# A fifth batch's first half by seven block products, and one of its block sums made by two DMA loads

## The chip, the cores and the metric

One core of one Trainium2 chip runs the whole program. The metric is the device time of one execution in microseconds; the median of the runs shown counts. Everything is in float32 with matmuls of split operands, as described below.

## The reference

The input `x` has 8 batches of 1024 rows and 512 columns; `cond` has one row of 512 per batch. Two layers, each with a residual, follow each other:

```python
# L0: a layer matrix with a low-rank part that depends on the batch
ae = _layernorm(ada_emb, ln_g, ln_b)
h = gelu(ae @ w1 + b1, approximate=False)
x_a, x_b = split(h @ w2 + b2, 2)           # per batch: 512 x 8 each
layer = base_layer[None] + einsum('bdr,bkr->bdk', x_a, x_b)
x = x + einsum('btc,bco->bto', x, layer)
# L1: a matrix scaled by the condition on both sides
ys = y / sqrt(512)
d = rsqrt(einsum('bi,io->bo', ys * ys, weight * weight) + 1e-8)
x = x + einsum('bsi,io->bso', x * ys[:, None, :], weight) * d[:, None, :]
```

So each batch's output is its 1024x512 block of `x` times one 512x512 matrix, P_b.

## The kernel before

The kernel first makes the eight matrices P_b (in the code `q[b]`, and `ph[b]`, `pl[b]` split in two), and then multiplies. Each float32 operand is split into a rounded high part (ScalarE casts it) and the rest (VectorE, DVE in the profile, subtracts), and a product is three matmuls: high x high, high x rest, rest x high.

A batch has two halves of 512 rows, a half has four tiles of 128. The common way is `main(b, t)`: one tile of 128 rows is twelve 128x512 matmuls (`po`), an eviction by ScalarE (`o`) and a store on ScalarE's queue. The halves' inputs come in by `load_x` on SyncE's queue (1 MB), are split by `split_x` into `xs`, and the matrices are split by `split_p`.

The last halves are done in another way, by the class `Seven`: a half is cut in 2x2 blocks, and seven block products replace eight (Winograd's scheme). `make_sums` makes the right sums T1 to T4 of one batch's matrix (tile `traw`, rounded to `th`, rests in `tl`), `make_right` splits the matrix itself, and `make_left` makes the left sums S1 to S4 of one half (`sraw`, `sh`, `sl`) and the split blocks `xa` and `x22`. The raw sums of both kinds share one buffer, with the tag `sums`. `part(g, steps, ...)` issues the seven products in the order 1, 5, 6, 2, 7, 3, 4, the evictions between them, and after each product one step of the generator `make_left` of the next half, so that the next half is prepared while this one is multiplied. The PSUM banks are named `sw`, `sz` and `sv` in the profile. The bank `sw` holds product 1, and products 6, 7 and 4 are added onto it; the sum after product 6 is copied out by ScalarE, the one after product 7 is added by DVE, the one after product 4 is copied by ScalarE:

```python
            for p in self.ORDER:
                key = {5: "z", 3: "z", 2: "v"}.get(p, "w")
...
                    if p == 1:
                        se.copy(bank["v"][0][:, to], u)
                    elif p in (3, 7):
                        ve.tensor_add(o[:, to, cols], u, o[:, to, cols])
                    else:
                        se.copy(o[:, to, cols], u)
```

Before the change, five halves go by `Seven`: the second half of batch 5 (called 5_1 here) and both halves of 6 and 7. 44 tiles go by `main`: tiles 0 to 43, where tile i is batch i // 8, tile i % 8 of it.

What runs beside a tile is written down by hand: `at(*place(i), f, ...)` puts a step behind tile i. While `InOrder.on` is false, which it is from the first tile to the last, a scheduler may reorder the steps on ScalarE and DVE by priority; within the parts of `Seven` they stand as written. Each engine then runs its queue in order. SyncE carries the x loads and the stores of the parts, ScalarE the stores of the tiles, GpSimd (POOL) small loads earlier in the program.

Of the kernel before, what the change touches and what calls it, by code (L numbers as in the profile page):

```python
# [7 lines left out]
F32 = mybir.dt.float32  # L8
F32R = mybir.dt.float32r
AF = mybir.ActivationFunctionType  # L10
ALU = mybir.AluOpType
# [3 lines left out]
P = 128  # L15
NB = 8
# [14 lines left out]
def cond_resid_kernel(ctx: ExitStack, tc: tile.TileContext, small, cond, condrows, consts,  # L31
# [10 lines left out]
    nc = tc.nc  # L42
# [9 lines left out]
    class InOrder:  # L52
# [4 lines left out]
        def __init__(self, engine):  # L57
            self.engine = engine
# [5 lines left out]
    ve, se, sy = InOrder(nc.vector), InOrder(nc.scalar), InOrder(nc.sync)  # L64
# [14 lines left out]
    def big_tile(name, dtype=F32):  # L79
        return big.tile([P, KC, D], dtype, tag="big", name=name)  # L80
# [126 lines left out]
    r, t = newton_rsqrt(ve_l, sd, [NB, 1], "l")  # L207
# [86 lines left out]
    r, t = newton_rsqrt(v, sv, [P, KC, NB], "d")  # L294
# [15 lines left out]
    def work_tile():  # L310
        turns[0] += 1
        return work[:, turns[0] % KC, :]
# [61 lines left out]
    a11, a21 = b_raw[:, 0:2, 0:HD], b_raw[:, 0:2, HD:D]  # L374
    a12, a22 = b_raw[:, 2:4, 0:HD], b_raw[:, 2:4, HD:D]
# [158 lines left out]
    fold, pools = {}, {}  # L534
# [184 lines left out]
    def load_x(b, h):  # L719
        raw[b, h] = big_tile(f"x_{b}_{h}")  # L720
        sy.dma_start(raw[b, h], x[b, h])

    def split_x(b, j, part=None):

        t = raw[b, j // 2][:, :, (j % 2) * 2 * P:(j % 2 + 1) * 2 * P]
        if part != 1:
            xs[b, j] = big.tile([P, 2, KC, 2 * P], F32R, tag="big", name=f"xs_{b}_{j}")
            se.copy(xs[b, j][:, 0], t)
        if part != 0:
            hi, lo = xs[b, j][:, 0], xs[b, j][:, 1]  # L730
            ve.tensor_sub(lo, t, hi.bitcast(F32))
# [49 lines left out]
    two = Pair(2, False)  # L781
# [123 lines left out]
    class Seven:  # L905
# [9 lines left out]
        ORDER = (1, 5, 6, 2, 7, 3, 4)  # L915

        def __init__(self, b):
            self.b, self.left, self.right = b, {}, {}

        def make_sums(self):  # L920

# [32 lines left out]
                                  (3, slice(2, 4), slice(HD, D))):  # L954
                self.right[p] = ph[b][:, rows, cols], pl[b][:, rows, cols]

        def make_left(self, g):

            b, late = self.b, pools["late"]
            top, low = (raw[b, g][:, :, 2 * P * i:2 * P * (i + 1)] for i in range(2))  # L960
            a11, a12, a21, a22 = top[:, 0:2], top[:, 2:4], low[:, 0:2], low[:, 2:4]
            s = late.tile([P, 4, 2, 2 * P], F32R, tag="sl", name=f"sl_{b}_{g}", bufs=2)
            h = late.tile([P, 4, 2, 2 * P], F32R, tag="sh", name=f"sh_{b}_{g}", bufs=2)
            x = late.tile([P, 2, 2, 2 * P], F32R, tag="x22", name=f"x22_{b}_{g}", bufs=2)
            xa = big.tile([P, 2, KC, 2 * P], F32R, tag="big", name=f"xa_{b}_{g}")
            raws = late.tile([P, 4, 2, 2 * P], F32, tag="sums", name=f"sraw_{b}_{g}", bufs=1)
            s1, s2, s3, s4 = (raws[:, i] for i in range(4))
            self.left[g] = {5: (h[:, 0], s[:, 0]), 6: (h[:, 1], s[:, 1]), 7: (h[:, 2], s[:, 2]),
                            3: (h[:, 3], s[:, 3]), 4: (x[:, 0], x[:, 1]),
                            1: (xa[:, 0, 0:2], xa[:, 1, 0:2]), 2: (xa[:, 0, 2:4], xa[:, 1, 2:4])}  # L970

            def rest(two):
                ve.tensor_sub(s[:, two], raws[:, two], h[:, two].bitcast(F32))

            se.copy(xa[:, 0], top)
            se.copy(x[:, 0], a22)
            ve.tensor_add(s1, a21, a22)
            ve.tensor_sub(s2, s1, a11)
            yield
            se.copy(h[:, 0:2], raws[:, 0:2])  # L980
            ve.tensor_sub(s3, a11, a21)
            ve.tensor_sub(s4, a12, s2)
            yield
            se.copy(h[:, 2:4], raws[:, 2:4])
            ve.tensor_sub(xa[:, 1], top, xa[:, 0].bitcast(F32))
            yield
            rest(slice(0, 2))
            yield
            ve.tensor_sub(x[:, 1], a22, x[:, 0].bitcast(F32))
            yield  # L990
            rest(slice(2, 4))
            yield

        def product(self, g, p, banks, first):
# [53 lines left out]

    def late_pools():
        making.close()  # L1050
        pools["o"] = ctx.enter_context(tc.tile_pool(name="opool2", bufs=3))
        pools["late"] = ctx.enter_context(tc.tile_pool(name="late", bufs=1))

    NTT = NT // P
    after = {}

    def at(b, t, f, *args):
        after.setdefault((b, t), []).append((f, args))
# [5 lines left out]
    place = lambda i: divmod(i, NTT)  # L1064
# [9 lines left out]
    for b, spots in ((4, [11 + n for n in spread]), (6, [21 + n for n in spread])):  # L1074
# [3 lines left out]
        for n, p in enumerate(Pair.ORDER):  # L1078
            spot = spots[2 * n]
# [14 lines left out]
    def all_left(seven, g):  # L1094
        for _ in seven.make_left(g):
# [12 lines left out]
    TILES = (NB - 2) * NTT - NTT // 2  # L1108
    for i in range(TILES):
        b, t = divmod(i, NTT)  # L1110
        if t == 0 and b + 1 < NB - 2:
# [86 lines left out]
```

## Time and profile before

| what | value |
|---|---|
| median of 3 runs | 294.06 us (293.88 to 294.23) |
| profiled execution | 293.74 us, of it the span 291.9 us |
| TensorE busy | 286.3 us, 98% of the span |
| DVE, ScalarE, GpSimd busy | 214.8, 175.0, 35.9 us |
| granted TensorE clock | 0.998 |

The span is what the trace shows, from the first instruction to the last; the time of an execution is 1.84 us longer. All times below in the form 226.94 are microseconds from the span's start. In a group of the profile, `out<-in` names the tiles by the program's names with the numbers left out, and a time in brackets is how long the engine had been idle and what it waited for. Instructions issued through the helpers `mm` and `InOrder` all stand at the helper's line, so they are told apart by their tiles.

### The profile page before, as it was taken

To read this page: it belongs to the slowest core of one execution; us is meant where nothing else is said; L and a number is where in the kernel's file an instruction comes from. 1 tells how busy PE (TensorE), PEld (TensorE's weight loads), DVE (VectorE), ACT (ScalarE), POOL (GpSimd) and SP (SyncE) were. 2 spreads that over 40 slices of the span, in tenths; PEclk is the share of its full clock that TensorE was granted. 3 is DMA by queue.
4 is the path that set the end of the run, shared out by engine and by line. 5 is a ranking of instruction groups with operands and counts; after the bars stand their busy time and mean duration, and the time that the engine had idled before them with its cause. 6 is when DMAs were issued, how large, how long until landed. Compare 5 with 4: busy or idle time off the path is not lost.

```text
span 291.9 us, 4100 instructions
## 1 busy us (share of the span) xinstructions
PE 286.3 (98%) x1519; PEld 225.2 (77%) x1519; DVE 214.8 (74%) x295; ACT 175.0 (60%) x272; POOL 35.9 (12%) x77
## 2 busy tenths in 40 slices
PE   7999999999999999999999999999999999999995
PEld 3665566467877878888877888887888889999994
DVE  2889898989916999519799565326789977798912
ACT  5757263286849884658654575544658745856641
POOL 2111000202944560000022000000000000000000
PEclk9999999999999999999999999999999999999999
DMA  7999999992799783332328114262175870852334
GB/s 209 405 429 413 411 403 405 390 383 90 187 321 322 235 250 116 110 145 93 159 80 263 55 72 135 83 216 74 72 251 176 291 257 1 290 204 87 142 146 144
DMA packets 19924, 62.14 MB, mean 213 GB/s; under 512 B 2736, under 2 KB 4016, under 8 KB 15552
## 3 DMA queue, kind: packets, MB, share of 16 engines
q1 hardware_dynamic: 9504, 43.76, 40.7%
q10 hardware_dynamic: 6912, 12.32, 11.5%
q0 software_dynamic: 3488, 5.79, 7.5%
q8 instruction: 12, 0.20, 0.3%
q14 instruction: 8, 0.07, 0.1%
HBM read 44.02 MB, written 17.84 MB: 212 GB/s over the span
## 4 chain that ended last, share of the span: by engine, by line
PE 96%; DMA 2%; ACT 0%; DVE 0%; SPq 0%; ACTq 0%; issue 0%
PE po L45 42%; PE pp L45 20%; PE sw L45 9%; PE px L45 5%; PE sz L45 5%; PE pg L45 4%; PE pq L45 4%; PE sv L45 2%; DMA b_raw<-in_baseT 2%; PE pr L45 1%; PE pt_t L45 1%; PE ps_t L45 0%; PE pq_v L45 0%; PE pq_z L45 0%; ACT o L62 0%; DVE o L62 0%
## 5 line engine op out<-in xcount | busy, mean ns | idle before, releaser
L45 PE MATMUL po<-ph,xs 128*128 128x512 f32 x352 | 113.7, 392 | 0.0
L45 PEld LDWEIGHTS po<-ph,xs 128*128 128x128 f32 x352 | 66.0, 188 | 15.6 <-issue 1.7
L45 PE MATMUL po<-pl,xs 128*128 128x512 f32 x176 | 68.6, 390 | 0.0
L62 ACT COPY o<-po 128x512 f32<-128x512 f32 x44 | 25.9, 588 | 35.0 <-PE po L45 35.0
L45 PEld LDWEIGHTS po<-pl,xs 128*128 128x128 f32 x176 | 33.0, 188 | 6.7
L62 DVE TENSOR_TENSOR xs<-x,xs 128x1024 fp32r<-128x1024 f32 (+1 forms) x23 | 27.0, 1176 | 15.0 <-ACT xs L62 15.0
L62 DVE TENSOR_TENSOR nl_p<-n,nh_p 128x1024 fp32r<-128x1024 f32 x21 | 25.7, 1222 | 12.4 <-ACT nh_p L62 12.4
L62 ACT CAST nh_p<-n 128x1024 fp32r<-128x1024 f32 x21 | 22.1, 1054 | 14.6 <-DVE n L62 10.9
L62 ACT CAST xs<-x 128x1024 fp32r<-128x1024 f32 x22 | 23.0, 1056 | 3.6 <-DMA x<-in_x 3.6
L62 ACT COPY q<-pp 128x512 f32<-128x512 f32 x30 | 17.4, 586 | 8.7 <-PE pp L45 8.6
L542 POOL DMA_DIRECT2D fa<-kept_a x28 | 13.8, 508 | 58.3 <-PE pr L45 54.0
L45 PE MATMUL pp<-nh_p,sh 128*128 128x512 f32 x48 | 19.0, 396 | 0.0
L45 PE MATMUL pp<-nh_p,sl 128*128 128x512 f32 x48 | 18.7, 390 | 0.0
L45 PE MATMUL pp<-nl_p,sh 128*128 128x512 f32 x48 | 18.7, 390 | 0.0
L62 DVE SCALAR_TENSOR_TENSOR n<-w_sb,ysT,d 128x512 f32<-128x512 f32 x24 | 16.9, 748 | 0.9 <-DMA d<-d_out 0.9
L62 ACT CAST sh<-sraw 128x1024 fp32r<-128x1024 f32 (+1 forms) x14 | 12.9, 926 | 6.8 <-DVE sraw L62 6.8
L62 DVE TENSOR_TENSOR sl<-sraw,sh 128x1024 fp32r<-128x1024 f32 (+1 forms) x14 | 14.9, 1067 | 2.2 <-ACT sh L62 2.2
L62 DVE TENSOR_TENSOR pl<-q,ph 128x1024 fp32r<-128x1024 f32 (+1 forms) x10 | 11.1, 1116 | 6.9 <-ACT ph L62 6.9
L45 PE MATMUL px<-w,hT 128*32 128x512 f32 x128 | 15.6, 599 | 0.0
L62 ACT COPY o<-sw 128x512 f32<-128x512 f32 (+1 forms) x12 | 6.2, 518 | 15.4 <-PE sw L45 12.3
L62 DVE TENSOR_TENSOR q<-pr,q 128x512 f32<-128x512 f32 x14 | 8.8, 688 | 7.9 <-PE pr L45 7.8
L62 DVE TENSOR_TENSOR n<-n,n 128x1024 f32<-128x1024 f32 x12 | 14.5, 1225 | 0.1
(199 smaller groups left out, 576.6 us busy)
## 6 DMA issues: line engine op xcount, KB each, us to landing
w<-in_w SPq DMA_DIRECT2D x16, 1024.0 KB, 10.4
x<-in_x SPq DMA_DIRECT2D x16, 1024.0 KB, 5.6
out<-o ACTq DMA_DIRECT2D x44, 256.0 KB, 2.3
out<-o SPq DMA_DIRECT2D x8, 512.0 KB, 2.9
fa<-kept_a POOLq DMA_DIRECT2D x28, 64.0 KB, 2.7
ft<-kept_t POOLq DMA_DIRECT2D x28, 64.0 KB, 3.5
d<-d_out POOLq DMA_DIRECT2D x6, 256.0 KB, 7.3
w_sb<-in_w SPq DMA_DIRECT2D x1, 1024.0 KB, 8.5
```

The lines of the kernel that those rows point to most:

```text
L45: tc.keep_in_program_order(nc.tensor.matmul(*args, **kw))
L62: return lambda *a, **kw: pin(f(*a, **kw)) if InOrder.on else f(*a, **kw)
L542: nc.gpsimd.dma_start(fold[name, b][32 * c:32 * c + 32, :], kept[name, g][32 * i:32 * i + 32, :])
```

## The change

The first half of batch 5 (5_0) goes by seven products as well: 40 tiles go by `main`, six halves by `Seven`. The left sum S1 = A21 + A22 of each of the six halves is no longer added by DVE; `load_sum` loads A21 from the input in DRAM to a tile `s1` of its own (one buffer) and then A22 onto it, in an accumulating DMA, both on GpSimd's queue. The load of the next half's S1 is issued within `make_left`, once this half's S1 has been read. The steps of `make_left` are put in another order, with the casts and rests of single sums apart. Batch 5's matrix is split by `make_right` (three quarters of it) rather than `split_p`; the right sums of 5, 6 and 7 are made behind tiles 32, 37 and 38; `make_right` of batch 6 moves into part 5_0. The output tiles in the late stage have two buffers rather than three.

```diff
+        def load_sum(self, g):
+
+            xg = x[self.b, g]
+            s1 = pools["late"].tile([P, 2, 2 * P], F32, tag="s1", name=f"s1_{self.b}_{g}", bufs=1)
+            nc.gpsimd.dma_start(s1, xg[:, 0:2, 2 * P:])
+            nc.gpsimd.dma_start(s1, xg[:, 2:4, 2 * P:], accum_op=ALU.add)
+            self.s1[g] = s1
...
-        def make_left(self, g):
+        def make_left(self, g, following=None):
...
-            s1, s2, s3, s4 = (raws[:, i] for i in range(4))
+            s1, (s2, s3, s4) = self.s1.pop(g), (raws[:, i] for i in range(1, 4))
...
             se.copy(xa[:, 0], top)
             se.copy(x[:, 0], a22)
-            ve.tensor_add(s1, a21, a22)
+            ve.tensor_sub(s3, a11, a21)
+            yield
+            ve.tensor_sub(xa[:, 1], top, xa[:, 0].bitcast(F32))
+            se.copy(h[:, 2], s3)
+            ve.tensor_sub(x[:, 1], a22, x[:, 0].bitcast(F32))
+            yield
+            se.copy(h[:, 0], s1)
             ve.tensor_sub(s2, s1, a11)
             yield
-            se.copy(h[:, 0:2], raws[:, 0:2])
-            ve.tensor_sub(s3, a11, a21)
             ve.tensor_sub(s4, a12, s2)
+            se.copy(h[:, 1], s2)
+            ve.tensor_sub(s[:, 0], s1, h[:, 0].bitcast(F32))
+            se.copy(h[:, 3], s4)
+            if following:
+                following[0].load_sum(following[1])
             yield
-            se.copy(h[:, 2:4], raws[:, 2:4])
-            ve.tensor_sub(xa[:, 1], top, xa[:, 0].bitcast(F32))
+            rest(slice(1, 3))
             yield
-            rest(slice(0, 2))
-            yield
-            ve.tensor_sub(x[:, 1], a22, x[:, 0].bitcast(F32))
-            yield
-            rest(slice(2, 4))
+            rest(slice(3, 4))
             yield
...
-        pools["o"] = ctx.enter_context(tc.tile_pool(name="opool2", bufs=3))
+        pools["o"] = ctx.enter_context(tc.tile_pool(name="opool2", bufs=2))
...
-    for b, spot in ((4, 27), (5, 33)):
-        for j in range(2):
-            at(*place(spot + j), split_p, b, j)
+    for j in range(2):
+        at(*place(27 + j), split_p, 4, j)
...
-    at(*place(34), s5.make_sums)
-    at(*place(34), s5.share_right)
-    at(*place(35), s6.make_sums)
-    at(*place(37), s7.make_sums)
-    at(*place(38), load_x, NB - 3, 1)
-    at(*place(39), all_left, s5, 1)
-    at(*place(41), s6.make_right)
-    at(*place(42), load_x, NB - 2, 0)
-
-    TILES = (NB - 2) * NTT - NTT // 2
+    at(*place(32), s5.load_sum, 0)
+    at(*place(33), load_x, NB - 3, 0)
+    at(*place(32), s5.make_sums)
+    at(*place(34), s5.make_right)
+    at(*place(35), all_left, s5, 0, (s5, 1))
+    at(*place(36), load_x, NB - 3, 1)
+    at(*place(37), s6.make_sums)
+    at(*place(38), s7.make_sums)
+
+    TILES = (NB - 3) * NTT
...
+    load_x(NB - 2, 0)
+    s5.part(0, s5.make_left(1, (s6, 0)), then=s6.make_right)
     load_x(NB - 2, 1)
-    s5.part(1, s6.make_left(0))
+    s5.part(1, s6.make_left(0, (s6, 1)))
     load_x(NB - 1, 0)
-    s6.part(0, s6.make_left(1))
+    s6.part(0, s6.make_left(1, (s7, 0)))
     load_x(NB - 1, 1)
-    s6.part(1, s7.make_left(0), then=s7.make_right)
+    s6.part(1, s7.make_left(0, (s7, 1)), then=s7.make_right)
     s7.part(0, s7.make_left(1))
     s7.part(1, last=True)
```

In the queues as built, the right sums of batches 6 and 7 stand on DVE behind the left sums of 5_0; the casts of 6's are on ScalarE behind the eviction of tile 38; those of 7's stand in part 5_0, behind the `sv` copy of product 1 and ahead of the cast of S3 of 5_1, which itself stands ahead of the copy that follows product 6.

More of the change, by code (lines that the diff above doesn't have):

```diff
@@ L917, in __init__ @@
         def __init__(self, b):
-            self.b, self.left, self.right = b, {}, {}
+            self.b, self.left, self.right, self.s1 = b, {}, {}, {}
+        def load_sum(self, g):
[4 more added lines that the diff above has]
+            self.s1[g] = s1
         def make_sums(self):
@@ L970, in make_left, with rest @@
                             1: (xa[:, 0, 0:2], xa[:, 1, 0:2]), 2: (xa[:, 0, 2:4], xa[:, 1, 2:4])}
-            def rest(two):
-                ve.tensor_sub(s[:, two], raws[:, two], h[:, two].bitcast(F32))
+            def rest(at):
+                ve.tensor_sub(s[:, at], raws[:, at], h[:, at].bitcast(F32))
             se.copy(xa[:, 0], top)
             se.copy(x[:, 0], a22)
-            ve.tensor_add(s1, a21, a22)
+            ve.tensor_sub(s3, a11, a21)
[5 more added lines that the diff above has]
+            se.copy(h[:, 0], s1)
             ve.tensor_sub(s2, s1, a11)
             yield
-            se.copy(h[:, 0:2], raws[:, 0:2])
-            ve.tensor_sub(s3, a11, a21)
             ve.tensor_sub(s4, a12, s2)
+            se.copy(h[:, 1], s2)
[3 more added lines that the diff above has]
+                following[0].load_sum(following[1])
             yield
-            se.copy(h[:, 2:4], raws[:, 2:4])
-            ve.tensor_sub(xa[:, 1], top, xa[:, 0].bitcast(F32))
+            rest(slice(1, 3))
             yield
-            rest(slice(0, 2))
-            yield
-            ve.tensor_sub(x[:, 1], a22, x[:, 0].bitcast(F32))
-            yield
-            rest(slice(2, 4))
+            rest(slice(3, 4))
             yield
@@ L1087, in cond_resid_kernel, with all_left @@
         at(*place(end + 1), rank_term, b + 1)
-    for b, spot in ((4, 27), (5, 33)):
-        for j in range(2):
-            at(*place(spot + j), split_p, b, j)
+    for j in range(2):
+        at(*place(27 + j), split_p, 4, j)
     s5, s6, s7 = (Seven(NB - i) for i in (3, 2, 1))
-    def all_left(seven, g):
-        for _ in seven.make_left(g):
+    def all_left(seven, g, following):
+        for _ in seven.make_left(g, following):
             pass
     at(*place(31), late_pools)
-    at(*place(34), s5.make_sums)
-    at(*place(34), s5.share_right)
-    at(*place(35), s6.make_sums)
-    at(*place(37), s7.make_sums)
-    at(*place(38), load_x, NB - 3, 1)
-    at(*place(39), all_left, s5, 1)
-    at(*place(41), s6.make_right)
-    at(*place(42), load_x, NB - 2, 0)
-    TILES = (NB - 2) * NTT - NTT // 2
+    at(*place(32), s5.load_sum, 0)
[7 more added lines that the diff above has]
+    TILES = (NB - 3) * NTT
     for i in range(TILES):
         b, t = divmod(i, NTT)
-        if t == 0 and b + 1 < NB - 2:
+        if t == 0 and b + 1 < NB - 3:
             p_tiles(b + 1)
```

## The prediction

> **What bounds the kernel now.** I read the page first, for the chain of waits and the busy shares.
>
> ```profile
> span 291.9 us, 4100 instructions
> PE 286.3 (98%) x1519; PEld 225.2 (77%) x1519; DVE 214.8 (74%) x295; ACT 175.0 (60%) x272; POOL 35.9 (12%) x77
> PE 96%; DMA 2%; ACT 0%; DVE 0%; SPq 0%; ACTq 0%; issue 0%
> ```
>
> TensorE is the path: 96% of the chain. So an edit gains only by taking matmul time away, and it costs whatever it makes TensorE wait. Next the busy time by stretch: the last eight tiles of batch 4, the four tiles that the change removes, then halves of seven products.
>
> ```profile
> 205.18:226.94 21.76, 21.76 (x97) 18.02 (x96) 18.98 (x22) 15.24 (x19) 0.00 (x0) 1.00 0.53 179
> 226.94:237.82 10.88, 10.88 (x49) 9.01 (x48) 10.81 (x15) 7.08 (x10) 0.00 (x0) 1.00 0.88 300
> 237.82:247.89 10.07, 10.07 (x86) 10.07 (x85) 6.18 (x8) 5.99 (x9) 0.00 (x0) 1.00 0.13 49
> 257.97:268.05 10.08, 10.08 (x87) 10.08 (x86) 8.23 (x11) 7.46 (x11) 0.00 (x0) 1.00 0.56 210
> ```
>
> The columns are length, then busy PE, PEld, DVE, ACT, POOL, clock, DMA share, GB/s. TensorE never stops, at full clock. A half by tiles takes 10.88 us, by products 10.07. But DVE is busy 29.8 of the 32.6 us ahead of 237.82: the work that prepares the first product half (5_1) and the right sums fills it. That is the stretch from which the change takes 10.88 us.
>
> **The gain.** 48 matmuls of 128x512 go, 84 of 128x256 come: 10.88 - 10.07 = 0.81 us off the path, and nothing more, since nothing else stands on it.
>
> **What the first product half now finds.** Part 5_0 starts at 237.82 - 10.88 = 226.94. Of its time I need this: a product is twelve matmuls, 10.07 / 7 = 1.44 us, in the order 1, 5, 6, 2, 7, 3, 4. Products 1, 6, 7 and 4 add up in one PSUM bank, and ScalarE must copy the sum after product 6 out before product 7 adds to it. So that copy is due by 226.94 + 4 x 1.44 = 232.70. Even now the cover is thin: in half 5_1 it ends at 242.83 + 0.59 = 243.42, and product 7 starts at 243.57.
>
> ```profile
> 242.83 0.59 ACT L62 COPY o<-sw 128x512 f32<-128x512 f32 x1
> ...
> 215.76 1.29 DVE L62 TENSOR_TENSOR traw<-q 128x512 f32<-128x512 f32 x2
> 216.97 1.41 DVE L62 TENSOR_TENSOR traw<-q,traw 128x512 f32<-128x512 f32 x2
> 218.77 2.36 DVE L62 TENSOR_TENSOR tl<-traw,th 128x1024 fp32r<-128x1024 f32 x2 [0.39 <-ACT th L62]
> 221.17 0.69 DVE L62 TENSOR_TENSOR traw<-q 128x512 f32<-128x512 f32 x1
> ```
>
> The DVE rows are one set of right sums (batch 6 now): 221.17 - 215.76 = 5.41 us from its first subtraction to the next set's, two rounding casts on ScalarE in between. There are two ways up to the copy, and both must be walked.
>
> By ScalarE: in the new order the casts of batch 6's right sums stand behind the eviction of tile 38 (batch 4's tile 6). Evictions of batch 4 begin at 208.10, 210.82, so 2.72 apart; tile 38's begins at 208.10 + 6 x 2.72 = 224.42. Then: eviction 0.5 to the next start, first cast 1.05, so DVE's two rests at 226.0, 2.4 us, to 228.4. The set for batch 7 shares the one buffer `sums` and follows: 5.41, to 233.8. Only then DVE starts S3 of half 5_1, 0.72, to 234.53. ScalarE's cast of that S3 (0.52 to the next start) stands ahead of the copy: 235.06 + 0.62 = 235.68. Product 7 waits 235.68 - 232.70 = 2.98 us.
>
> By DVE: its split of batch 4's last x quarter waits for ScalarE's cast behind tile 34's eviction (213.54) and ends at 216.3; then the left block of 5_0, six 128x512 at 0.605 and two 128x1024 at 1.14, 6.0 us with one dependent pair, to 222.3; then batch 6's four subtractions, 2.6, to 224.9. That is the moment ScalarE gets to their cast by the other way (224.42 + 0.5). Both agree, so the stall does not hang on one guess. It needs `x_5_0` (issued 210.8 in both kernels, about 5.3 on the way) and S1 of 5_0 by 216.
>
> Two small waits follow. DVE's add of product 7 comes behind S2, S4 and the rest of S1, and holds product 4 by about 0.25. Before part 7_0 the right split of batch 7 (1.74 us of DVE) sits between other rests and costs about 0.2. Sum of waits: 2.98 + 0.25 + 0.20 = 3.43.
>
> **S1 by DMA.** Removed are DVE adds of 0.60 each, off the path. Added are two 256 KB loads in a row on GpSimd's queue, the second adding to what the first left, so it waits for its landing. S1 has one buffer: the next pair starts when S2 and the rest of S1 have read it, which is S2 0.72, S4 0.60, rest 0.72, together 2.04 us after a landing. The cycle is 2.04 + both loads, against a half of 10.07: it is hidden as long as both take up to 8.03 us. For 5_0 the first load waits for the store of tile 31 (208.0), so 216 is met with up to 8 us as well. Beyond that, every microsecond is paid once in each of four cycles and in part also before product 7, 4 to 5 us in all. GpSimd's queue holds nothing else there (POOL 0.00 above); behind a late S1, ScalarE has a cast that blocks copies out of PSUM, DVE has S2. No accumulating load is in the trace. The nearest rows, from the DMA issues in the windows 60 to 70, 100 to 115 and 85 to 95 us:
>
> ```profile
> kept_a<-st_a POOLq DMA_DIRECT2D x1, 256.0 KB, 3.4
> ...
> d<-d_out POOLq DMA_DIRECT2D x2, 256.0 KB, 4.1
> ...
> x<-in_x SPq DMA_DIRECT2D x1, 1024.0 KB, 7.2
> ...
> fa<-kept_a POOLq DMA_DIRECT2D x4, 64.0 KB, 5.4
> ```
>
> Two plain loads would be 6.8 by the first, 8.2 by the second, in which two shared the queues. The last two rows are the warning: a load of 64 KB under an x load takes 5.4 and lands with it. Low end 6.8, high end 2 x 7.3 = 14.6 (the page's median for `d`, while weights stream). I take 7.5, between the nearest two: hidden, by 0.5 us. An accumulation that costs 2 us more than a plain load would undo that.
>
> [...]
>
> **Edits with small prices.** Output tiles go from three buffers to two: an eviction then waits for the store two tiles back. A store takes 2.2 us, or 5.4 under an x load (the window 222 to 224 has one); the new order puts the x load of 6_0 at about 221.2, just after tile 36's store (219.9). At 5.4 that store lands at 225.3, and tile 38's eviction, the head of the long chain, moves from 224.42 by 0.9. Bounds 0 and 0.9; I take 0.4, since the store starts first. The right split of batch 5 is 3/4 as large and the one of batch 6 moves into part 5_0 behind product 7: counted on DVE, off the path, where later halves have room (DVE 8.2 of 10.07 us). The S1 rows in part 5_1 and later run with 0.4 us to spare at product 7's copy, so no other half stalls unless the loads do.
>
> **The sum.** -0.81 + 3.43 + 0.4 = +3.0. The profiled execution took 293.74 (span 291.9 and 1.84 around it), so 296.7 in its terms; the median of the runs is 294.06, 0.32 above, which gives 297.1.
>
> **The rivals.** (1) The load cycle decides: both loads take 9.2 us rather than 7.5. Then each cycle is 1.2 us short, 4 to 5 us per us, on top of the sum: about 302.5; at 11 us over 310. For it: the accumulation reads its target too, and the 5.4 us row; against it: only one x load runs per half. It decides from 8.0 us on. Between 8.0 and 9.4 the time runs from 297 to 304.
> (2) Faster: the first half does not stall, and 10.88 becomes 10.07: 294.06 - 0.81 = 293.25. The point from which it decides is DVE's S3 of 5_1: it must start 3 us earlier, by 230.8, which asks for batch 7's right sums to fit ahead of it. DVE's 29.8 us of work in 32.6 speaks for room that could be used better; against it stands the order written into both queues, and the eviction that times the chain.
> (3) The stall is there but only about 2.3, with the small waits gone and no store late: 294.06 - 0.81 + 2.3 = 295.6. The rows are the same on both ways, so I give it little.
>
> **How the numbers follow.** The forecast (loads hidden, stalls of 2.5 to 4) has 0.53, rival 1 up to 304 has 0.25, beyond 304 0.16, rival 3 0.03, rival 2 0.03. The range 295.9 to 304 takes in the bounds of the store (0 and 0.9) and the loads up to 9.4 us, and leaves out about 0.2. Slower by over 0.2% (0.6 us, about what a measurement of this kernel can tell from no change): 0.95; faster 0.03, from rival 2; same 0.02, the low tail of rival 3.
>
> **What would show it.** In the profile after: TensorE idle near 232.7 for about 3 us, released by ScalarE's copy `o<-sw`, with `traw`/`tl` of batch 7 on DVE just before; po matmuls 480 rather than 528; `s1` loads landing in 3 to 5 us and GpSimd idle between them. If instead TensorE stops in every half and the releaser goes back to the `s1` landing, rival 1 holds. If TensorE runs through from 226.9 to 287, rival 2 does, and my order of the queues is read wrongly.

## The result and the profile after

| | before | after |
|---|---|---|
| median | 293.97 us (293.76 to 294.23) | 311.94 us (311.11 to 316.15) |
| profiled execution, its span | 293.74, 291.9 | 311.11, 309.3 |
| granted TensorE clock | 0.998 | 0.972 |

The change costs 18.0 us: ratio 1.0601, 95% interval 1.0578 to 1.0625. The time lies above the whole forecast range. The median and the range count all four executions; the ratio leaves out the one of 316.15 us, over 1.5% above the fastest. First the page of the changed kernel, the lines that answer to those of before, and the row of the granted clock over 40 slices of the span:

```profile
span 309.3 us, 4226 instructions
...
PE 292.4 (95%) x1555; PEld 232.2 (75%) x1555; DVE 216.7 (70%) x303; ACT 178.1 (58%) x287; POOL 48.3 (16%) x89
...
PEclk9999999999999999999999999999995799959999
...
PE 77%; DMA 12%; DVE 6%; ACT 2%; issue 2%; SPq 0%; ACTq 0%; DVEq 0%
```

TensorE is no longer the whole path: DMA has 12% of the chain, VectorE 6%. TensorE is busy for 6.1 us more, with 0.81 us less to do, and in some slices of the last third its clock is 5 and 7 tenths. Two things happen: TensorE stops, and after the stops it works at half speed. The busy time by stretch shows both (length, busy PE, PEld, DVE, ACT, POOL, granted clock, DMA share, GB/s):

```profile
227.16:229.92 2.76, 2.76 (x25) 2.75 (x23) 2.33 (x4) 0.00 (x0) 0.58 (x1) 1.00 0.92 366
229.92:232.75 2.83, 0.28 (x3) 0.07 (x1) 0.00 (x0) 0.97 (x2) 0.00 (x0) 1.00 0.98 234
232.75:239.58 6.83, 3.81 (x18) 3.81 (x19) 5.78 (x7) 5.44 (x8) 0.00 (x0) 0.50 0.21 79
239.58:243.00 3.42, 0.99 (x8) 0.79 (x7) 3.39 (x5) 2.22 (x6) 0.00 (x0) 1.00 0.00 0
243.00:246.40 3.40, 3.38 (x16) 3.38 (x17) 2.87 (x5) 3.06 (x5) 0.60 (x1) 0.50 0.00 0
...
271.40:277.13 5.73, 5.73 (x27) 5.73 (x28) 2.97 (x4) 0.79 (x2) 1.58 (x2) 0.50 0.59 204
```

At full clock 2.76 us hold 25 matmuls of 128x256; at 0.50, 5.73 us hold 27. The account from the starts of the matmuls (a stop is the step between two starts, less the usual 0.12 us):

| place | stop | work at half clock behind it | lost by it (half) |
|---|---|---|---|
| ahead of product 6 of 5_0, 229.92 to 235.78 | 5.74 | 3.81 | 1.90 |
| ahead of product 7 of 5_0, 240.30 to 243.02 | 2.60 | 3.38 | 1.69 |
| ahead of product 4 of 6_0, 267.52 to 271.40 | 3.76 | 5.73 | 2.87 |

Sum 12.10 + 6.46, and with the gain of 0.81 off, 17.75. The last matmul begins at 305.86 instead of 288.09: 17.77 later. So the account is closed. Only the stop in the middle row was forecast.

What TensorE waited for last, and ScalarE's two longest waits ahead of the first stop, are in these rows (in the first three: us in total, times, longest):

```profile
PE sw L45 <- ACT sv L62: 5.6, 1, 5.6
PE sw L45 <- DVE o L62: 3.6, 1, 3.6
PE sw L45 <- ACT o L62: 2.4, 1, 2.4
...
220.24 0.62 ACT L62 CAST sh<-s 128x512 fp32r<-128x512 f32 x1 [4.93 <-DMA s<-in_x]
...
231.78 0.59 ACT L62 COPY o<-po 128x512 f32<-128x512 f32 x1 [5.52 <-DMA out<-o]
```

Product 6 waits for ScalarE's `sv` copy of product 1, product 4 for VectorE's add of product 7, product 7 for ScalarE's copy of the sum after product 6. Where each comes from is read in the chain of waits, in order of time (start, length, what):

```profile
209.40 2.92 DMA s<-in_x
212.61 7.60 DMA s<-in_x
220.24 0.63 ACT sh L62
...
225.16 6.54 DMA out<-o
231.78 0.59 ACT o L62
...
241.14 0.70 DVE sraw L62
...
242.39 0.59 ACT o L62
243.02 2.93 PE sw L45 x12
...
256.18 5.33 DMA s<-in_x
261.80 6.90 DMA s<-in_x
268.72 0.70 DVE sraw L62
...
270.66 0.69 DVE o L62
```

The first stop has its root at 212.61. The adding load of S1 of 5_0 lies beside the load of `x_5_0` (issued 211.04) and then that of `x_5_1` (issued 216.59), and takes 7.60 us: S1 lands at 220.21, where the forecast needed it by 216 (its first load also went out 1.4 us later than forecast, at 209.40). ScalarE's cast of S1 and all evictions behind it are late, and the store of tile 36 goes out only at 225.16, together with the load of `x_6_0` (225.20) and just ahead of the adding load of 5_1's S1 (226.54). It lands after 6.54 us, and with two output tiles the eviction of tile 38 waits for it until 231.78, where the forecast had 224.42. All that follows is some 7 us late: behind that eviction stand two casts, the eviction of tile 39 and only then the `sv` copy, at 235.15. The third stop is a pair of S1 loads of 12.5 us (256.18 to 268.70), beside the loads of `x_6_1` and `x_7_0`.

### The profile page after: what moved, and what is told of

Its sections match the earlier page's. It is cut to its first block, busy times and chain, and to the rows that moved or that the text cites. A ratio compares the mean times of both kernels' runs of the same rounds, so it can differ in the third digit from the quotient of the medians.

```text
span 309.3 us, 4226 instructions
## 1 busy us (share of the span) xinstructions
PE 292.4 (95%) x1555; PEld 232.2 (75%) x1555; DVE 216.7 (70%) x303; ACT 178.1 (58%) x287; POOL 48.3 (16%) x89
## 4 chain that ended last, share of the span: by engine, by line
PE 77%; DMA 12%; DVE 6%; ACT 2%; issue 2%; SPq 0%; ACTq 0%; DVEq 0%
PE po L45 29%; PE pp L45 19%; PE sw L45 8%; DMA s<-in_x 7%; PE px L45 5%; PE pg L45 4%; PE pq L45 4%; PE sz L45 3%; DMA out<-o 3%; DVE sraw L62 2%; DVE tl L62 1%; DMA b_raw<-in_baseT 1%; PE sv L45 1%; PE pr L45 1%; ACT o L62 1%
## 5 line engine op out<-in xcount | busy, mean ns | idle before, releaser
L45 PE MATMUL po<-ph,xs 128*128 128x512 f32 x320 | 103.9, 393 | 0.0
L45 PEld LDWEIGHTS po<-ph,xs 128*128 128x128 f32 x320 | 60.0, 188 | 14.4 <-issue 1.7
L45 PE MATMUL po<-pl,xs 128*128 128x512 f32 x160 | 62.4, 390 | 0.0
L62 ACT COPY o<-po 128x512 f32<-128x512 f32 x40 | 23.5, 588 | 36.6 <-PE po L45 31.1
L62 DVE TENSOR_TENSOR xs<-x,xs 128x1024 fp32r<-128x1024 f32 (+1 forms) x21 | 24.5, 1171 | 15.2 <-ACT xs L62 15.2
L45 PEld LDWEIGHTS po<-pl,xs 128*128 128x128 f32 x160 | 30.0, 188 | 6.1
L45 PE MATMUL sw<-th,sh 128*128 128x256 f32 x48 | 15.0, 312 | 8.0 <-ACT sv L62 5.6
L924 POOL DMA_DIRECT2D s<-in_x x6 | 4.4, 738 | 102.6 <-DVE pl L62 53.9
L62 ACT CAST sh<-sraw 128x512 fp32r<-128x512 f32 x22 | 13.0, 617 | 8.1 <-DVE sraw L62 8.0
L45 PEld LDWEIGHTS sw<-th,sh 128*128 128x128 f32 x48 | 10.2, 213 | 8.4 <-ACT sv L62 5.8
## 6 DMA issues: line engine op xcount, KB each, us to landing
w<-in_w SPq DMA_DIRECT2D x16, 1024.0 KB, 10.1
```

The lines of the kernel that those rows point to most:

```text
L45: tc.keep_in_program_order(nc.tensor.matmul(*args, **kw))
L62: return lambda *a, **kw: pin(f(*a, **kw)) if InOrder.on else f(*a, **kw)
L924: nc.gpsimd.dma_start(s1, xg[:, 0:2, 2 * P:])
```

## The experiments

All times are compared with runs of the kernel before on the same chip. Kernels with long stops scatter by up to three per cent between executions (308.2 to 317.0 us in the run without the two stores).

### Which part costs what

**Six halves without loads of S1.** S1 back on VectorE, three output tiles, all else as changed.

```diff
-            nc.gpsimd.dma_start(s1, xg[:, 0:2, 2 * P:])
-            nc.gpsimd.dma_start(s1, xg[:, 2:4, 2 * P:], accum_op=ALU.add)
...
-            s1, (s2, s3, s4) = self.s1.pop(g), (raws[:, i] for i in range(1, 4))
+            s1, s2, s3, s4 = (raws[:, i] for i in range(4))
...
+            ve.tensor_add(s1, a21, a22)
...
-        pools["o"] = ctx.enter_context(tc.tile_pool(name="opool2", bufs=2))
+        pools["o"] = ctx.enter_context(tc.tile_pool(name="opool2", bufs=3))
```

> The changed kernel with S1 added by VectorE again, as the second operation on VectorE of each half's sums, without loads of S1 and with three output buffers; the first half of batch 5 still goes by seven products. Theory A (the loads of S1 carry all of the loss but the predicted stop ahead of product 7 of 5_0): no late store, stops of 3.5 to 4.0 us and 0.5 to 1.0 us ahead of products 7 and 4 of 5_0, with up to 1.8 us of half clock behind them: 297.0 to 300.0 us. Theory B (six halves are too much for VectorE in this stage, with or without loads): stops in 6_0 and later as well, 303 us or more.

Measured 298.98 us, ratio 1.0162 (1.0144 to 1.0179): theory A. One stop is left, ahead of product 7 of 5_0, and TensorE's waits have one row:

```profile
PE sw L45 <- ACT o L62: 4.0, 1, 4.0
```

The stop is 4.19 us, and half clock behind it loses 3.07 us, more than the 1.8 of theory A; the wait ahead of product 4 that A also had did not show.

**The loads without the sixth half.** Five halves as before, S1 by loads, the new order of the left sums, two output tiles.

Of its difference to the kernel before, the lines of the schedule:

```diff
     at(*place(38), load_x, NB - 3, 1)
-    at(*place(39), all_left, s5, 1)
+    at(*place(36), s5.load_sum, 1)
+    at(*place(39), all_left, s5, 1, (s6, 0))
```

> The kernel before, with S1 of its five halves made by the two loads, the new order of the steps of the left sums and two output buffers; the first half of batch 5 goes by tiles as before, and the right sums and splits stay where they were. Theory A (loads of S1 that lie beside a 1 MB load of x take 5.3 to 7.6 us each, and the cycle of one half doesn't hide a pair of them): stops of TensorE in the middle of 6_0 of 2 to 4 us with half clock behind them, 297 to 301 us. Theory B (the loads are hidden as long as the first half of batch 5 goes by tiles, and all of the loss is of that half): 293.8 to 294.6 us, no stop over 0.3 us.

Measured 307.01 us, 1.0459 (1.0423 to 1.0495): B falls, and A's sum was too small. Stops of 4.94, 3.46 and 0.70 us, and 3.37 us lost to half clock. Most of the loss, 13.1 of the 18 us, comes without the sixth half. The first stop stands behind a tile's store of 6.81 us (236.37 to 243.17), beside the load of `x_6_1` and an S1 load. For the second the chain shows the cycle of S1 turning by itself:

```profile
254.14 6.49 DMA s<-in_x
...
260.65 0.70 DVE sraw L62
...
262.07 0.61 DVE sl L62
...
262.97 2.92 DMA s<-in_x
...
266.18 8.07 DMA s<-in_x
```

Read S1 (S2, S4, rest: 2.0 us), load, adding load: from landing (260.63) to landing (274.25) 13.6 us, where a half has 10.07.

**Two output tiles alone.** The kernel before, with one line changed:

```diff
-        pools["o"] = ctx.enter_context(tc.tile_pool(name="opool2", bufs=3))
+        pools["o"] = ctx.enter_context(tc.tile_pool(name="opool2", bufs=2))
```

> The kernel before with two output tiles in the late stage instead of three, and nothing else. Theory A (two buffers cost only where loads of S1 lie beside a load of x and a store): 293.8 to 294.4 us, no stop of TensorE over 0.5 us. Theory B (the stores that wait beside the 1 MB loads of x are enough to hold up evictions, as the 5.1 us stop of the run with five halves by loads behind a store of 6.8 us suggests): a stop of 1 to 5 us in the stage of the last tiles, 295 to 299 us.

294.70 us, 1.0030 (1.0015 to 1.0044): between the two theories, nearer to A. ScalarE waits 6.9 us in all for stores, up to 2.7 each, but TensorE's longest stop is 0.4 us. By the medians it costs 0.6 us, within the forecast's bounds for this edit, 0 and 0.9.

### The loads of S1

**No accumulation.**

```diff
-            nc.gpsimd.dma_start(s1, xg[:, 2:4, 2 * P:], accum_op=ALU.add)
+            nc.gpsimd.dma_start(s1, xg[:, 2:4, 2 * P:])
```

> The changed kernel with A22 loaded over A21 instead of added to it in the second load of S1 (S1 is then A22 alone): the same bytes, queue and order, without accumulation. Theory A (the load of x beside it is what makes it slow): the second loads that lie beside a load of x still take over 5 us, and the time is 305 to 311 us, at most the 1.0 us by which the quiet loads differ (3.9 and 2.9) better in each of some four halves. Theory B (accumulation is the price): all loads of S1 take 2.9 to 3.5 us, the stop ahead of product 6 of 5_0 and the one in 6_0 are gone, 296 to 299 us.

307.90 us, 1.0494 (1.0445 to 1.0544): theory A. Beside a load of x the plain second load takes 6.3, 7.2, 5.7 and 7.0 us, in quiet stretches 3.2 and 3.3. So neighbourhood, not accumulation, makes them slow. The accumulation costs some 3 to 4 us of the 18 (3.1 by the ratios, whose intervals nearly touch, 4.0 by the medians); in the quiet it is 0.7 us a load (3.9 for 3.2), and that the rest is what this sets off is argued, not shown.

**S1 two halves ahead.** S1 of 6_0 and 7_0 goes to output tiles that are free after the last tiles; each load from 6_0 on is issued a half earlier.

```diff
+            if g == 0 and self.b > NB - 3:
+                s1 = pools["o"].tile([P, D], F32, tag="o", name=f"s1_{self.b}_{g}")
...
+    s6.load_sum(0)
     load_x(NB - 2, 0)
-    s5.part(0, s5.make_left(1, (s6, 0)), then=s6.make_right)
+    s5.part(0, s5.make_left(1, (s6, 1)), then=s6.make_right)
...
-    s5.part(1, s6.make_left(0, (s6, 1)))
+    s5.part(1, s6.make_left(0, (s7, 0)))
```

> The changed kernel with the S1 loads of 6_0, 6_1, 7_0 and 7_1 issued a half earlier: S1 of 6_0 and 7_0 goes to an output tile that is free after the last tiles, so that a pair of loads has some 20 us instead of some 8. Theory A (the cycle read S1, load 2.9 us, load 4 to 9 us is longer than a half): the stops in 6_0 and later and the half clock behind them are gone, about 6.5 us; the ones ahead of products 6 and 7 of 5_0 stay: 304 to 307 us. Theory B (these loads take their time from the loads of x and the stores wherever they stand): stops over 1 us remain in 6_0 or later, 308 us or more.

305.07 us, 1.0381 (1.0361 to 1.0400): theory A. No stop over 0.3 us from 6_0 on, though the last adding load takes 10.1 us beside a load of x: it is late for nobody. The stops ahead of products 6 and 7 of 5_0 stay (6.75 and 2.05 us).

**And S1 of batch 5 without loads**, added by GpSimd from the x that is in SBUF:

```diff
-    at(*place(32), s5.load_sum, 0)
...
+            if b == NB - 3:
+                gp.tensor_tensor(s1, a21, a22, ALU.add)
```

> The run with S1 two halves ahead, with S1 of the two halves of batch 5 added by GpSimd from the x that is already in SBUF instead of loaded; the loads for 6_0 and later stay a half ahead. Theory A (the pair of S1 loads beside the loads of x_5_0 and x_6_0 starts the chain that stops TensorE ahead of product 6 of 5_0): that stop (6.9 us) and the half clock behind it are gone, the stop ahead of product 7 is 3 to 4.5 us with up to 1.8 us of half clock: 298 to 301 us. Theory B (the late stores and the two output buffers make that stop without loads as well): a stop over 3 us ahead of product 6, 303 us or more.

302.88 us, 1.0301 (1.0286 to 1.0317), between A's and B's numbers: the stop ahead of product 6 falls from 6.75 to 2.05 us, but half clock follows both that and the 4.26 us ahead of product 7. The loads carry two thirds of the first stop. What is left stands under two output tiles, and evictions still wait for stores there (2.7 us at most); GpSimd's additions take 1.42 and 1.75 us, and what they add is not told apart.

**The two late stores left out** (tiles 36 and 37).

```diff
-        nc.scalar.dma_start(out[b, t * P:(t + 1) * P, :], o)
+        if (b, t) not in ((4, 4), (4, 5)):
+            nc.scalar.dma_start(out[b, t * P:(t + 1) * P, :], o)
```

> The changed kernel without the stores of tiles 36 and 37 (those output rows stay unwritten). Theory A (a chain: the accumulating load of S1 of 5_0 beside the load of x_5_0 makes the evictions late, the store of tile 36 then goes out beside the load of x_6_0, and with two output buffers the eviction of tile 38 waits for it): the eviction of tile 38 comes at 224 to 226 instead of 231.8, the stop of TensorE ahead of product 6 of 5_0 (5.7 us) is gone, and with it the half clock that followed it (1.9 us); the stop ahead of product 7 stays between 2.5 and 3.0 us, and the one in 6_0 (3.8 us) stays: 302.5 to 304.5 us. Theory B (the loads of S1 are late by themselves, whatever the output buffers do): the stop ahead of product 6 stays over 4 us and the time is 311 to 312 us.

312.65 us, 1.0587 (1.0509 to 1.0664), executions from 308.2 to 317.0: neither theory's time. The evictions of tiles 37 and 38 stand together at 226.44, the second ahead of 227.6 instead of at 231.78, and the first stop shrinks from 5.74 to 3.27 us, where A had it gone and B over 4. What is left follows S1: it lands at 220.97, and ScalarE's cast `th` waits for VectorE's right sums of batch 6 until 229.58. And the time does not follow even that: ahead of product 7 there are 2.94 us, later 3.91 and 2.76 us, and half clock behind all four. What one stop gives back, the late S1 loads of the next half take.

**Three output tiles**, with the parts' own tiles at three for the room.

```diff
-        pools["o"] = ctx.enter_context(tc.tile_pool(name="opool2", bufs=2))
+        pools["o"] = ctx.enter_context(tc.tile_pool(name="opool2", bufs=3))
...
-            o1, o2 = (pools["late"].tile([P, 2, D], F32, tag="o2", name=f"o{i}_{b}_{g}", bufs=4)
+            o1, o2 = (pools["late"].tile([P, 2, D], F32, tag="o2", name=f"o{i}_{b}_{g}", bufs=3)
```

> The changed kernel with three output tiles in the late stage, as before the change; to make room the parts' own output tiles are three instead of four. Theory A (with two output tiles the eviction of tile 38 waits for the late store of tile 36): that eviction comes 3 us or more earlier, the stop ahead of product 6 of 5_0 shrinks from 5.7 us to 2.5 to 3.5 us, as without the two stores; the stop in 6_0 stays: 307 to 311 us. Theory B (the late evictions alone make the stop, the store waits add nothing): the stop stays over 5 us, 311 us or more.

Executions from 308.3 to 314.8 us, ratio 1.0537 (1.0492 to 1.0582): no clear answer on the time. In the profiled one, the longest of the four, the eviction of tile 38 begins at 227.62, 4 us earlier, and still TensorE stops for 4.1 us, between A's 2.5 to 3.5 and B's 5. So the store is one link, some 1.6 to 2.5 us of the first stop. In its other part ScalarE's cast `th` waits for the right sums until 229.71, as in the run without the two stores.

### The stop that was forecast

**Right sums of batch 7 behind part 5_1**, in the changed kernel, then in the kernel without loads:

```diff
-    at(*place(38), s7.make_sums)
...
+    s7.make_sums()
     load_x(NB - 1, 0)
```

> The changed kernel with the right sums of batch 7 made behind part 5_1 instead of behind tile 38. Theory A (the prediction's step: these 5.4 us of VectorE work stand ahead of S3 of 5_1, and so of the copy that product 7 of 5_0 waits for): the stop ahead of product 7 (2.6 us) and the half clock behind it (1.7 us) are gone, the stop ahead of product 6 (5.7 us) stays, and up to 1.7 us come back where the sums now stand: 307.5 to 309.5 us. Theory B (the stop ahead of product 7 is only the tail of the late store, as all queues are 7 us late by then): it stays at 2 us or more, 311 to 313 us.

310.04 us, 1.0572 (1.0505 to 1.0640), executions from 309.2 to 313.8. The stop ahead of product 7 is gone, as A said, and 1.74 us come back in 6_0. But the profiled execution, the longest of the four, has 6.81 us ahead of product 6 and 4.56 us in 6_1, both behind late loads: under the loads this run can't price the step.

> The run of six halves without loads of S1 (S1 on VectorE, three output buffers), with the right sums of batch 7 made behind part 5_1 instead of behind tile 38. Theory A (the prediction's step: those 5.4 us hold up S3 of 5_1 and so product 7 of 5_0): the stop of 4.3 us ahead of product 7 and the half clock behind it are gone; of it 1.7 us come back ahead of a product of 6_0, where the sums now stand, and 0.5 us behind that: 295.3 to 296.5 us. Theory B (VectorE has so much to do up to the end of 6_0 that the stop only moves): a stop of 3 us or more in 6_0, 298 us or more.

295.67 us, 1.0059 (1.0046 to 1.0072): theory A. The stop of 4.19 us is gone, clock 1.0 up to the last matmul, and what comes back is named in TensorE's waits:

```profile
PE sw L45 <- ACT sv L62: 1.6, 1, 1.6
```

A stop of 1.74 us in 6_0 where 1.7 was forecast. The forecast step is shown.

### The half clock

**The stops filled with matmuls**, into a bank that product 5 starts anew:

```diff
+    FILL = {(5, 0): 72, (6, 0): 32}
...
+                if p == 5 and (b, g) in FILL:
+                    (lh, _), (rh, _) = self.left[g][1], self.right[1]
+                    for _ in range(FILL[b, g]):
+                        mm(bank[key][0][:, 0, :], lh[:, 0, 0:P], rh[:, 0, :], start=True, stop=True)
```

> The changed kernel with 72 matmuls of 128x256 more ahead of product 5 of 5_0 and 32 ahead of product 5 of 6_0, into the bank that product 5 then starts anew: 8.6 and 3.8 us of TensorE work at 0.12 us each, about as much as the stops that stand behind them (5.7 and 2.6 us, 3.8 us). Theory A (TensorE runs at half clock because it had stopped): no granted clock of 0.5 in the records, stops under 1 us, and with 12.5 us of work more the time falls by the 6.5 us that the half clock cost, to 304.5 to 307 us. Theory B (the half clock has another cause, the stops only coincide with it): half clock stays, 311 us or more. If the stops don't shrink by what is filled in, both give 315 to 324 us.

315.76 us, 1.0752 (1.0707 to 1.0797). A's time is missed: stops of 1.76, 1.69, 0.98 and 3.66 us come behind the filling, three of them ahead of a product that waits for VectorE's add, one behind a copy by ScalarE. The time is that of the last sentence above, and by itself it decides nothing. But where the three stops were filled there is no half clock, and only the 3.66 us have some (1.71 us lost, 6.46 without filling; the mean granted clock is 0.995 rather than 0.972). So A is right on the clock.

**Stops made on purpose** in the kernel before, by chains of casts on GpSimd:

```diff
+    HOLD = {(5, 1): 14, (6, 0): 18, (6, 1): 24}
...
+                if p == 2 and (b, g) in HOLD:
+                    t = pools["late"].tile([P, HD], F32R, tag="hold", name=f"hold_{b}_{g}", bufs=1)
+                    for _ in range(HOLD[b, g]):
+                        pin(nc.gpsimd.tensor_copy(t, o1[:, 0, 0:HD]))
```

> The kernel before with three stops of TensorE made on purpose, of rising length: behind product 2 of 5_1, 6_0 and 6_1 a chain of 14, 18 and 24 casts of 128x256 on GpSimd starts (396 ns each in the profile of before), and one matmul ahead of product 1 of the next part reads its result. With 3.7 us of products beside each chain, stops of about 2, 3.5 and 6 us, some 11.5 us in all. Theory A (the granted clock falls to 0.5 when TensorE has stopped for nearly 3 us, and for a while after): no half clock behind the shortest stop, half clock of 3.4 us or more behind the other two, and 1 to 4 us of time more than the stops add up to. Theory B (half clock comes from something else in the changed kernel): no granted clock of 0.5 ahead of the last matmul, and the time is that of before and the sum of the stops, within 0.5 us.

326.07 us, 1.1094 (1.1076 to 1.1113): the casts take 559 ns each rather than 396, so the stops are 6.06, 7.48 and 11.46 us, too long to show where it begins. All three have half clock behind them: 5.33, 5.70 and 5.34 us of work, 8.19 us lost. Account: 25.0 + 8.19 + 0.36 for three added matmuls is 33.55; the last matmul begins 33.35 us later. Hence the shorter chains of 5, 6 and 8 casts:

> The kernel before with three stops made on purpose, with chains of 5, 6 and 8 casts on GpSimd instead of 14, 18 and 24. From the stops of 6.06, 7.48 and 11.46 us of the longer chains, each cast is worth some 0.54 us: stops of about 1.2, 1.0 to 1.6 and 2.7 us. Theory A (half clock from a stop of about 2 us on): none behind the first two, half clock for 3.4 us behind the third; 294 us and the sum of the stops, and 1.4 to 2.0 us more. Theory B (the other stops had half clock because queues were late around them): no half clock, the time is that of before and the stops' sum.

300.21 us, 1.0213 (1.0197 to 1.0230): theory A. The first chain makes no stop of over 0.5 us, the others make 1.02 and 3.16. Sum 1.02 + 3.16, 1.71 for the half clock and 0.36 for the added matmuls: 6.25; the time is 6.23 us longer. The stretches (length, busy engines, clock):

```profile
258.28:259.30 1.02, 0.16 (x3) 0.00 (x1) 0.99 (x2) 0.59 (x1) 0.97 (x1) 1.00 0.54 205
259.30:266.00 6.70, 6.70 (x56) 6.70 (x57) 4.84 (x6) 4.85 (x8) 0.00 (x0) 1.00 0.76 282
...
269.59:272.74 3.15, 0.15 (x2) 0.00 (x0) 3.12 (x5) 0.59 (x1) 2.91 (x4) 1.00 0.18 67
272.74:276.50 3.76, 3.76 (x19) 3.76 (x20) 2.39 (x4) 0.86 (x2) 0.00 (x0) 0.55 0.60 223
```

A stop of 1.02 us costs 1.02 us. One of 3.16 us costs 1.7 more.

### Is there a version that gains?

**Sums on GpSimd.** No loads of S1, three output tiles; GpSimd adds S1, makes batch 7's right sums in a buffer of their own and one of the rests.

```diff
-            ve.tensor_sub(x[:, 1], a22, x[:, 0].bitcast(F32))
+            gp.tensor_tensor(x[:, 1], a22, x[:, 0].bitcast(F32), ALU.subtract)
...
+            gp.tensor_tensor(s1, a21, a22, ALU.add)
...
+            for o, x, y in ((t1, b12, b11), (t2, b22, t1), (t3, b22, b12), (t4, b21, t2)):
+                gp.tensor_tensor(o, x, y, ALU.subtract)
```

> Six halves by seven products, without any load of S1 and with three output buffers: GpSimd adds S1 from x in SBUF, makes the four right sums of batch 7 in a buffer of their own while 5_0 is multiplied, and the rest of A22; the casts and rests of batch 7's right sums stand in the last two steps of 6_0's left sums, and batch 7's matrix is split a part earlier. VectorE has some 7 us less to do. Theory A (with VectorE unburdened no wait is left, and the 0.81 us of 84 matmuls of 128x256 for 48 of 128x512 come through): no stop over 0.3 us, 292.9 to 293.5 us. Theory B (GpSimd's own operations of 128x512 are much slower than the estimate of 1.2 to 1.8 us from its 0.49 us for 128x128, or hold up VectorE's): stops over 1 us in 5_0 to 6_1, 295 us or more.

300.47 us, 1.0241 (1.0219 to 1.0263): theory B, above all its second half. VectorE's groups by line and shape from 205 to 285 us (count, busy us, mean ns of one, idle before):

```profile
L62 DVE TENSOR_TENSOR xa<-x,xa 128x1024 fp32r<-128x1024 f32 x6 | 11.9, 1978 | 2.4 <-ACT xa L62 2.4
...
L62 DVE TENSOR_TENSOR sraw<-sraw,x 128x512 f32<-128x512 f32 x6 | 8.5, 1416 | 1.2 <-POOL sraw L62 1.2
```

And GpSimd's:

```profile
L62 POOL TENSOR_TENSOR x<-x,x 128x512 fp32r<-128x512 f32 x6 | 12.2, 2030 | 2.0 <-ACT x L62 2.0
L62 POOL TENSOR_TENSOR sraw<-x 128x512 f32<-128x512 f32 x6 | 10.5, 1754 | 91.9 <-DMA out<-o 61.2 <-DVE sl L62 19.0 <-ACT sv L62 7.0
```

GpSimd takes 1.75 to 2.03 us for one, at the end of the estimate and above. And VectorE's operations beside them stretch: the rest `xa` from 1223 ns in the kernel before to 1978, the subtraction from S1 from 692 to 1416. The work that left VectorE came back as longer operations. Why they lengthen, these rows don't show.

**Right sums of batch 7 in pieces.** From the kernel without loads: these sums get a buffer of their own and stand in six pieces in the steps of 5_1's, 6_0's and 6_1's left sums; batch 7's matrix is split in part 6_0. VectorE adds S1, but not that of 5_0: contrary to the sentence below, its two loads are in this kernel and in the next. They go to an output tile that is free early, are issued at 196.00 and 199.20 us and land by 203.24, 11 us ahead of their first use.

```diff
+            raws = big.tile([P, 4, 2, HD], F32, tag="big", name=f"traw_{b}")
...
+    s5.part(0, mixed(s5.make_left(1, (s6, 0)), sums7, 0, 5), then=s6.make_right)
...
+    s5.part(1, mixed(s6.make_left(0, (s6, 1)), sums7, 3, 4, 5))
...
+    s6.part(0, mixed(s6.make_left(1, (s7, 0)), sums7, 2), then=s7.make_right)
```

> The same kernel as the one with the loads of S1 for 6_0 and 6_1 in the quiet stretch, with all S1 added by VectorE, no load of S1 at all: 1.4 us more on VectorE. Theory A: stops of 0.4 to 0.7 us in 5_1 from the added work, 293.5 to 294.3 us, 0.2 to 0.7 us more than with the quiet loads. Theory B (loads cost something wherever they stand): this one is the faster of the two.

**And S1 of 6_0 and 6_1 by loads in the quiet stretch**, into output tiles that are free as well (the first line of the diff is in both kernels):

```diff
+            s1 = pools["o"].tile([P, D], F32, tag="o", name=f"s1_{self.b}_{g}")
...
+    s6.load_sum(0)
+    s6.load_sum(1)
     s5.part(0, mixed(s5.make_left(1, (s6, 0)), sums7, 0, 5), then=s6.make_right)
```

> Six halves by seven products, three output buffers, S1 added by VectorE but for 6_0 and 6_1: their S1 is loaded by the two pairs of loads to output tiles that are free after the last tiles, at about 235 to 246 us, between the load of x_6_0 and that of x_6_1. The right sums of batch 7 have a buffer of their own and stand in six pieces in the steps of 5_1's, 6_0's and 6_1's left sums; batch 7's matrix is split a part earlier. Theory A (loads of S1 in a quiet stretch cost nothing, and the predicted stop ahead of product 7 was all that stood against the gain of 0.81 us): each pair lands within 8 us, no stop over 0.5 us, 293.0 to 293.8 us. Theory B (VectorE is full in this stage, whatever the order): stops of 1 us or more between 230 and 260 us, 294.5 us or more.

Without the loads of 6_0 and 6_1 293.42 us, 0.9985 (0.9968 to 1.0002); with them **292.89 us, 0.9964 (0.9951 to 0.9977)**: 1.1 us less than before, the only version that is surely faster than both kernels. Theory A in both (each time 0.1 us under its range), and 0.5 us between them, as A had it; the longest stop is 0.41 us, in 5_1 of the first. One detail of A fails: the four loads are issued from 228.84 on and all have landed by 240.1, but a pair takes up to 10.5 us, since the two pairs run beside each other. Nobody waits for them. TensorE's waits in this stage are empty. Its page and two stretches:

```profile
span 290.9 us, 4217 instructions
...
PE 96%; DMA 1%; ACT 0%; DVE 0%; issue 0%; SPq 0%; ACTq 0%
```

```profile
226.94:237.00 10.06, 10.06 (x86) 10.02 (x85) 9.96 (x14) 7.88 (x14) 3.94 (x4) 1.00 0.41 125
237.00:247.10 10.10, 10.10 (x87) 10.10 (x86) 10.07 (x15) 8.38 (x13) 0.00 (x0) 1.00 0.85 248
```

VectorE is busy 9.96 of 10.06 and 10.07 of 10.10 us. Nothing more fits: a seventh half would have to bring its sums elsewhere.

## Why the prediction was wrong, step by step

- **The gain, 0.81 us: right.** The account of the changed kernel closes with it to 0.02 us, and once nothing waits the time falls by 1.1 us (0.7 to 1.4 by the interval; the last matmul begins 0.64 us earlier).
- **The stop ahead of product 7, 2.98 us: right in place and cause.** 2.60 us in the changed kernel, 4.19 without loads, and gone when batch 7's sums move. Without loads it begins at 233.09, forecast 232.70; in the changed kernel it came 7.7 us later than forecast, since the queues were late already. Of the two small waits the one of 0.25 us did not show, the one of 0.20 did.
- **S1 by DMA, "I take 7.5": this step failed.** In the quiet a pair takes 7.1 us (2.9, 0.3 to the next issue, 3.9), so the number was good for the quiet. Four of the six pairs lay beside a load of x and took 10.8, 9.8, 12.5 and 8.8 us, over the 8.03 up to which they were to be hidden. The prediction had the warning in its row of 5.4 us under a load of x, and put it aside with "only one x load runs per half". One per half is enough: the load of x goes out at the start of a part, when the buffers come free, and the S1 loads go out when S1 is read, in the same few microseconds (x at 225.20, 251.32, 260.23 and 275.44, the late pairs of S1 at 223.35, 256.18 and 271.05); ahead of 5_0 there are even two loads of x. Rival 1 named this mechanism and gave it 0.16 beyond 304 us. That its "over 310" at 11 us comes so close is in part luck: it counted every late microsecond once in each of four cycles and no half clock, while here two of the four late pairs set off the stops ahead of product 6 of 5_0 and product 4 of 6_0, the one of 8.8 us stopped nothing, and 6.46 us of the measured loss are half clock. "Hidden, by 0.5 us" should have been priced with the 5.4 us row (two make 10.8), not with the quiet ones.
- **Output tiles, 0.4 us, bounds 0 and 0.9: right alone, wrong in company.** Alone 0.6 us. In the changed kernel the eviction of tile 38 waits 5.5 us. The bounds were worked out with the evictions on time; they were late by the step above, and that late store fell on the load of `x_6_0` and an S1 load at once.
- **The half clock: left out altogether.** 6.46 of the 17.8 us. The prediction took a stop to cost its length. Behind the stop that it forecast rightly alone there are 1.69 us of it.

What stays open: how the first stop divides exactly between the late store and the late sums. Both follow from the late S1, and each cure moved the other; the runs give only bounds.

## What to carry to other kernels

Put a transfer that has a deadline where no large one runs, and price it by the rows that lie beside such a transfer, not by the quiet ones; one large load per cycle is enough if the same event lets both go: here four of the six pairs lay beside one and took 8.8 to 12.5 us, the two others 7.0 and 7.1. A stop of TensorE can cost more than its length: in the changed kernel those of 2.60, 3.76 and 5.74 us cost 1.69, 2.87 and 1.90 us more; in other runs stops of 1.02, 1.69 and 1.76 us cost their length alone. Where an engine's queue is full, cut the work that has no deadline (here a set of sums for two parts later) in pieces between the pieces that have one.

## What was not expected of the hardware

**Behind a stop TensorE works at half clock for microseconds.** In the changed kernel the granted clock is 1.0 or 0.5 from 200 us to the last matmul, and changes at 232.75, 239.58, 242.99, 246.41, 270.30 and 277.13: the stretches at half clock are 6.83, 3.42 and 6.83 us long. In the 3.41 us ahead of each of the three falls TensorE was busy for 0.87, 0.99 and 0.92 us; in the last 3.41 us at half clock it was busy for 3.42, 3.39 and 3.42 us, and full clock came back. With the short chains the clock is 1.00 over the 6.70 us behind the stop of 1.02 us, and 0.55 over the 3.76 us behind that of 3.16 us. From which length of stop on the clock falls is not shown: with S1 of batch 5 added by GpSimd half clock follows a stop of 2.05 us (mean clock 0.989), and none follows the 1.74 us in the kernel without loads whose right sums of batch 7 come later (0.999).

**Loads beside each other slow each other.** A load of 256 KB by GpSimd's queue takes 2.9 us in the quiet (3.9 adding) and 5.3 to 7.6 us beside the 1 MB load of x in the changed kernel, and that load takes 6.3 to 9.5 us instead of 5.6. In the run with S1 two halves ahead one adding load took 10.1 us. Stores lie beside them as well: without the two tile stores the adding load of 5_1 took 5.11 us rather than 6.64, beside the same load of x; and with the quiet loads, where late loads of x have stores alone beside them, they still take 6.5 to 7.4 us.
